# Ends of the 8-head graph-attention layers: free buffers and late denominators; the last projection's rows finished in groups of four

## The chip, the cores and the metric

The kernel runs on one core of a Trainium2 chip. A core has five engines with queues of their own: PE multiplies matrices into PSUM, DVE and ACT do elementwise work, POOL and SP here mainly issue DMA transfers (POOL also clears buffers). The metric is the device time of one launch in microseconds; lower is better. The median of three runs of the kernel before is 3410.56 us (3410.44 to 3414.77).

## The reference

Four layers follow each other on x (3327 rows, 512 columns) with one 0/1 matrix adj of 3327 x 3327. Each is x = layernorm(x + layer(x)) over the columns.

- Layers 0, 2 and 3 are graph attention with 8, 8 and 4 heads. For every head Wh = x W; the logit of row i against row j is leaky_relu(f1[i] + f2[j]), where f1 and f2 are products of Wh with two vectors; where adj[i, j] is 0 it is masked; softmax over j; the head's result is the softmax times Wh. Layers 2 and 3 end with elu.
- Layer 1 is a mean over neighbours: of each row's neighbours the first 64 in index order are kept, their rows are averaged and projected, passed through leaky_relu, set to 0 where a row has no neighbour, and added to leaky_relu of another projection of x.

```python
e = leaky_relu(f1[:, :, None] + f2[:, None, :], 0.2)
h = softmax(where(adj > 0, e, -9e15), axis=-1) @ Wh            # layers 0, 2, 3
keep = (A > 0) & (cumsum(A > 0, axis=1) <= 64)                 # layer 1
xj = leaky_relu((keep @ X) / max(cnt, 1) @ W_nb.T + b_nb)
x = layernorm(x + layer(x))
```

## The kernel before

The rows are padded to 26 tiles of 128 (NT = 26), in two halves of 13 (HALF). The transposed mask stays in SBUF as fp8 for the whole launch.

**The order of work.** PE's instructions keep the order in which the program writes them. On the other engines a scheduler orders the instructions when the program is built, except where `tc.keep_in_program_order` pins one. An engine runs its queue in order, so an instruction that waits holds everything behind it. Tiles come from pools with a number of buffers (`bufs`): a tile with the same name or tag waits until an older buffer has been read for the last time.

**An attention layer.** It begins with a projection (`project1`: four transposes of a row tile, copy `xT` on ACT; `project2`: 16 matmuls into `pw`, then `vt` on DVE, stored in DRAM as v). `prepare` and `cut` make the columns and rows of logits of one half, `rows` loads rows of logits broadcast over the partitions (`rb`, on POOL's queue). Then `unit` runs 8 times: for each half of the output columns i (1664 of them) and each slot s of 4 (two heads in an 8-head layer, one in layer 3). It walks over 26 tiles j: per head DVE makes the weights `t` (L402), ACT makes the fp8 tile `y` (L405), PE adds `t` times v into four banks `po` (L425), and for pairs of j adds the denominators into two banks `pd` (L377). At its end `po` goes to `ob`; `transposed` turns it by quads of four tiles (QUADS: 4, 4, 4, 1) on PE, copies it to `hb` on ACT (L457; two buffers) and stores it in DRAM as hd through SP (L458). That work is a list of jobs, one of which is taken at each j of the next unit. After the last unit what is left of the list is run at once; these are the ends of the layers.

**The denominators.** Per half, after slot 3 of the 8-head layers, the sums in `pd` lie in rows by piece and head. DVE transposes them in blocks of 32 (L486, L487) and adds pieces (`red`, L491). SP writes `red` to DRAM in four transfers with 32-byte pieces (`dd`, L495) and reads it back by row in one (`pes`, L498). `finish_sums` (L507 to L513, pinned for 8 heads) combines them on DVE into `rec`, the reciprocals. Layer 3 does so too, but after its very last unit it copies `pd` to `db`, and PE multiplies by a matrix of pieces (`sums`, L533) instead.

**Finishing rows.** `finish_steps` loads the row tiles h (from hd) and xr (the layer's input, always on POOL's queue), divides (L180), with elu takes exp on ACT (L185) and adds (L191, L192), otherwise adds (L194); `norm_rows` takes the statistics of all tiles of a group (L152, L153), the square root on ACT (L154), and scales on ACT (L161). Exp and square root use different tables of ACT, and a change of function between them brings a table load. The first two tiles are finished in the hook `ending`, ahead of the last `den` of the last unit.

**Sage (layer 1).** In its first part, for groups of two tiles, `finish` of the next group is issued, then `step1` (transposes L682, `xT` L684) and `step2` (16 matmuls `pz`, `pi`, L690 and L693; three bf16 parts of z, two in SBUF as `zs`, the third in DRAM as zd). In the second part `zl` is read back by 13 loads. For every block of 256 rows and every two tiles j, `pk` receives the carries `cy` (ACT, L762), PE adds the running count (L770), DVE makes the kept mask `kt` (L774), and PE adds three matmuls per tile j into `acc` (L809). `output` makes y (L782 on) with the counts `cnt`, which come from `cb`, a read of the counts in DRAM (L743 to L745), and the next layer's weights `wsb` are loaded on POOL (L730) for its projection, which begins behind tile 0. The counts `ctd` are made during layer 0 by `count_jobs` (`ct` L629, L632; `nb` L635).

**Layer 3's projection** (`third`) finishes rows in groups of two, each group's steps in one go ahead of the projections of the group before.

**Layer 0's projection** loads `xt` in three buffers on POOL's queue, interleaved with the loading of the mask; at t = 14 it runs `prepare`, `rows` and `cut` of half 0.

## Time and profile before

| what | us |
|---|---|
| median of three runs | 3410.56 |
| the profiled execution | 3407.9 |
| its span | 3406.2 |
| PE busy | 3262.8 (96%) |
| DVE busy | 2695.3 (79%) |
| ACT busy | 2351.4 (69%) |
| POOL busy | 214.7 (6%) |
| layer 0: projection, attention, end (from the start of the span) | 0 to 143, to 960.6, to 988.3 |
| sage: projections, turn, main part | to 1172, to 1193, to 1754 |
| layer 2: start, attention, end | to 1793, to 2562.7, to 2583 |
| layer 3: projection, attention, tail | to 2706, to 3380, to 3406.2 |

The profile is of one execution, and all its times are counted from the start of its span. A line such as L402 is a line of the kernel before. A busy PE is no proof of PE at its peak: its matmuls overlap, and their recorded ends are modelled, so the records of a stage are compared with records of the same shape in a stage where PE waits for nobody. PEld is PE's loading of weights, which runs beside the matmuls. A name with q (SPq) is the engine's own queue while it issues a transfer; `dd<-red` behind DMA is the transfer itself, from issue to landing. "A <- B" in a list of waits means that A stood idle until B had ended.

### The profile page before, as it was taken

To read this page: it belongs to the slowest core of one execution; us is meant where nothing else is said; L and a number is where in the kernel's file an instruction comes from. 1 tells how busy PE (TensorE), PEld (TensorE's weight loads), DVE (VectorE), ACT (ScalarE), POOL (GpSimd) and SP (SyncE) were. 2 spreads that over 40 slices of the span, in tenths; PEclk is the share of its full clock that TensorE was granted. 3 is DMA by queue.
4 is the path that set the end of the run, shared out by engine and by line. 5 is a ranking of instruction groups with operands and counts; after the bars stand their busy time and mean duration, and the time that the engine had idled before them with its cause. 6 is when DMAs were issued, how large, how long until landed. Compare 5 with 4: busy or idle time off the path is not lost.

```text
span 3406.2 us, 47019 instructions
## 1 busy us (share of the span) xinstructions
PE 3262.8 (96%) x18423; PEld 1631.0 (48%) x18423; DVE 2695.3 (79%) x2630; ACT 2351.4 (69%) x2128; POOL 214.7 (6%) x344
## 2 busy tenths in 40 slices
PE   8899999999989899999989999999997999999997
PEld 7544344444434345555544444444445754445453
DVE  5799999999967544444449999999997766668886
ACT  2388999999943233333338999899996755559885
POOL 3100000000010111111110000000001000000000
PEclk9899999999989999999999999999998999999998
DMA  9544111110143443333320111211107411122311
GB/s 372 214 127 123 52 49 53 42 49 28 38 123 128 116 111 87 90 85 85 85 81 26 41 50 48 56 44 47 35 25 225 169 41 42 41 51 79 95 42 48
DMA packets 313365, 284.65 MB, mean 84 GB/s; under 512 B 134253, under 2 KB 248631, under 8 KB 313144
## 3 DMA queue, kind: packets, MB, share of 16 engines
q1 hardware_dynamic: 280584, 170.27, 16.9%
q0 software_dynamic: 27040, 103.70, 9.5%
q10 hardware_dynamic: 5520, 7.69, 0.7%
q8 instruction: 145, 2.38, 0.3%
q14 instruction: 76, 0.62, 0.1%
HBM read 212.22 MB, written 69.35 MB: 83 GB/s over the span
## 4 chain that ended last, share of the span: by engine, by line
PE 79%; issue 7%; DVE 6%; DMA 4%; ACT 2%; POOL 0%; SPq 0%; ACTq 0%; POOLq 0%; DVEq 0%
PE po L425 49%; PE acc L809 9%; PE pd L377 7%; PE pw L268 5%; DVE t L402 4%; PE pz L690 3%; PE pi L693 3%; DMA raw<-in_adjT_dram 2%; ACT y L405 1%; PE pt L453 1%; DMA cy<-ctd 1%; PE pk L770 1%; PE pt L258 0%; PE pa L1022 0%; DVE mask L593 0%
## 5 line engine op out<-in xcount | busy, mean ns | idle before, releaser
L402 DVE SCALAR_TENSOR_TENSOR t<-rb,qc,mask 128x1664 f32<-128x1664 f32 x1040 | 1959.9, 1957 | 167.7 <-PE po L425 150.1
L405 ACT ACTIVATE y<-t,bi,sc 128x1664 fp8e4<-128x1664 f32 x1040 | 1771.1, 1766 | 317.3 <-PE pd L377 304.4
L425 PE MATMUL po<-t,vj 128*64 128x448 f32 (+3 forms) x8320 | 1924.6, 520 | 25.0 <-DVE t L402 22.3
L425 PEld LDWEIGHTS po<-t,vj 128*64 128x64 f32 (+1 forms) x8320 | 848.3, 148 | 978.2 <-issue 689.7
L809 PE MATMUL acc<-zs,kt 128*128 128x512 bf16 x1352 | 405.1, 382 | 0.0
L809 PEld LDWEIGHTS <-kt 128*128 128x128 fp8e4 x2028 | 199.1, 98 | 250.8 <-issue 9.5
L268 PE MATMUL pw<-wsb,xT 128*128 128x264 f32 (+1 forms) x1248 | 299.8, 395 | 9.2 <-DVE vt L274 7.5
L762 ACT CAST pk<-cy 128x512 f32<-128x512 bf16 x169 | 98.9, 587 | 294.5 <-DVE kt L774 251.1
L377 PE MATMUL pd<-y,sden 128*32 128x448 fp8e4 (+1 forms) x4160 | 259.4, 342 | 8.2 <-ACT y L405 8.2
L268 PEld LDWEIGHTS pw<-wsb,xT 128*128 128x128 f32 x1248 | 240.4, 196 | 53.4 <-issue 5.0
L809 PE MATMUL acc<-zl,kt 128*128 128x512 bf16 x676 | 257.8, 381 | 4.0 <-DMA zl<-zd 4.0
L774 DVE SCALAR_TENSOR_TENSOR kt<-pk,mask 128x512 fp8e4<-128x512 f32 x169 | 116.0, 687 | 99.7 <-PE pk L770 99.7
L377 PEld LDWEIGHTS <-sden 128*32 128x32 bf16 x4160 | 117.6, 96 | 160.3 <-issue 137.6
L274 DVE TENSOR_TENSOR vt<-pw,dc 128x256 f32<-128x256 f32 x156 | 59.0, 418 | 141.2 <-ACT dc L269 137.1
L356 POOL DMA_DIRECT2D rb<-r x40 | 21.9, 548 | 1617.0 <-DVE t L402 1604.5
L272 ACT COPY rc<-pw 128x8 f32<-128x8 f32 (+1 forms) x78 | 12.7, 163 | 138.7 <-PE pw L268 136.2
L690 PE MATMUL pz<-wn,xT 128*128 128x512 f32 x208 | 97.4, 613 | 10.1 <-ACT xT L684 10.1
L693 PE MATMUL pi<-wl,xT 128*128 128x512 f32 x208 | 93.5, 592 | 0.0
L659 POOL DMA_DIRECT2D cy<-ctd x91 | 67.9, 746 | 338.4 <-ACT pk L762 310.2
L782 DVE SCALAR_TENSOR_TENSOR y<-acc,cnt,bnb 128x512 f32<-128x512 f32 x26 | 19.5, 751 | 85.9 <-PE acc L809 85.9
L593 DVE TENSOR_SCALAR mask<-raw 128x832 fp8e4<-128x832 int32 (+2 forms) x90 | 53.1, 598 | 40.4 <-DMA raw<-in_adjT_dram 40.1
L154 ACT ACT_TABLE_LOAD x45 | 57.7, 1283 | 37.3 <-DVE mv L153 36.7
(177 smaller groups left out, 1661.6 us busy)
## 6 DMA issues: line engine op xcount, KB each, us to landing
vj<-v SPq DMA_DIRECT2D x312, 128.0 KB
rb<-r POOLq DMA_DIRECT2D x40, 832.0 KB, 4.6
raw<-in_adjT_dram SPq DMA_DIRECT2D x67, 416.0 KB
cy<-ctd POOLq DMA_DIRECT2D x78, 256.0 KB, 3.9
h<-hd SPq DMA_DIRECT2D x61, 256.0 KB
v<-vt SPq DMA_DIRECT2D x50, 256.0 KB
hd<-hb SPq DMA_DIRECT2D x48, 256.0 KB
xr<-x POOLq DMA_DIRECT2D x45, 256.0 KB, 3.2
```

The costliest lines, as they stand in the source:

```text
L268: nc.tensor.matmul(pw[e][:, :FW + H], xT[:, c, :], wsb[:, c, e, :], start=c == 0, stop=c == FC - 1)
L274: nc.vector.tensor_tensor(vt[:, hs, :], pw[e][:, :FW].rearrange("p (h d) -> p h d", d=D), self.dc[:, t, hs].rearrange("p (h e) -> p h e", e=1)
L377: nc.tensor.matmul(pd[c][32 * kk:32 * kk + 32, :w_], lhsT, rhs, start=(kk, c) not in seen, skip_group_check=final is not None, stop=last a ...
L402: nc.vector.scalar_tensor_tensor(t, rb[k], self.qc[:, j, h:h + 1], mask[:, j, i0:i0 + IW], op0=ALU.max, op1=ALU.mult)
L405: nc.scalar.activation(y, t, AF.Sigmoid, bias=self.bi[:, j, h:h + 1], scale=self.sc[:, j, h:h + 1], saturate=False)
L425: nc.tensor.matmul(po[c][k * D:(k + 1) * D, :z - a_], vj[:, j % 2, k * D:(k + 1) * D], ts[k][:, a_:z], start=j == 0, stop=j == NT - 1)
L659: nc.gpsimd.dma_start(out=cy[:, :n, :], in_=ctd[t:t + n, b * GW:(b + 1) * GW] .rearrange("(o t) i -> o t i", o=1).to_broadcast([P, n, GW]))
L690: nc.tensor.matmul(pz, xT[:, c, :], wn[:, c, :], start=c == 0, stop=c == FC - 1)
L693: nc.tensor.matmul(pi, xT[:, c, :], wl[:, c, :], start=c == 0, stop=c == FC - 1)
L762: nc.scalar.copy(pks[k % 2], carry[b, t // 4 * 4][:, t % 4:t % 4 + 2, :])
L774: nc.vector.scalar_tensor_tensor(kt, pk, NEIGHBOURS, mask[:, t:t + 2, i0:i0 + GW], op0=ALU.is_le, op1=ALU.mult, saturate=False)
L809: nc.tensor.matmul(acc, kts[t][:, s * P:(s + 1) * P], zs(t, c) if c < 2 else zl[:, t, :], start=t == 0 and c == 0, stop=t == NT - 1 and c ...
```

## The change

It has eight parts; line numbers with "after" are of the changed kernel.

1. `norm_rows` is split into `norm_steps`: the statistics of a tile follow its own addition, the square root and scaling follow for the group. `ending` receives the attention's pool: the xr tiles of the first two rows take buffers of the tag "hb", and in layer 2 the exp tile has two buffers.
2. In the last unit of an 8-head layer the last `hb` takes a buffer of "vj", and the third quad's takes that of "db".
3. Half 0 of the 8-head layers makes its denominators by PE: ACT copies `pd` to `db` in four copies, 13 matmuls follow as a job (`sums`), and two jobs later DVE's `reciprocals`.
4. Where the way over DRAM remains (half 1 of the 8-head layers; layer 3), `dd` is written in one transfer as it lies, and `place` reads it back with 16 transfers of 32-byte pieces. At the ends these go into `late`: in sage `place` is issued at t0 = 4 on SP's queue and `finish_sums` at t0 = 8, in layer 3's projection at groups k = 2 and 3. Within layer 3 `place` goes on POOL's queue at job 2 and `finish_sums` some jobs later. The columns rc are first copied into rec, and the first transpose is pinned.
5. `ct` is copied by ACT instead of DVE, and `nb` reads `ct` instead of PSUM.
6. In sage, `cy` has three buffers and two carries are loaded ahead; `cb` and `cnt` move into the first part; `finish` of the next group is issued after `step1` of the group's first tile; for tile 0 the third matmuls (`zl`) follow after all others; `wsb` is loaded on SP behind them.
7. Layer 3's projection finishes rows in groups 2, 2, 3, 4, 4, 4, 4, 3 and spreads their steps between the projections; h has 12 buffers for 10, xr 8 for 6.
8. Layer 0's projection has five `xt` buffers; `cut` comes at t = 14 as before without `rows` ahead of it, and `rows` comes at t = 20.

```diff
-    def norm_rows(pool, ys, t0):
-        n = len(ys)
+    def norm_steps(pool, ys, t0, n):
...
-                xr = pool.tile([P, F], F32, name="xr", bufs=xbufs)
+                xr = xpool.tile([P, F], F32, name="xr", tag="hb") if xpool else \
+                    pool.tile([P, F], F32, name="xr", bufs=xbufs)
...
+        def add_up(s):
+            add(s)
+            if not parts:
+                parts.extend(norm_steps(pool, ys, t0, n))
+            parts[0](s)
+
         steps.append(load)
         for s in range(n):
-            steps += [lambda s=s: divide(s), lambda s=s: add(s)]
-        steps.append(lambda: norm_rows(pool, ys, t0))
+            steps += [lambda s=s: divide(s), lambda s=s: add_up(s)]
+        steps.append(lambda: parts[1]())
...
-                ending()
+                ending(sp)
...
-                hb = sp.tile([P, 4, P], F32, name="hb")
+                if HS == 2 and half == 1 and s == NS - 1 and n < 4:
+                    hb = vp.tile([P, n, P], F32, name="hb", tag="vj")
+                elif HS == 2 and half == 1 and s == NS - 1 and s0 >= 8:
+                    hb = sp.tile([P, 4, P], F32, name="hb", tag="db", bufs=1)
+                else:
+                    hb = sp.tile([P, 4, P], F32, name="hb")
...
-            if not (final and s == NS - 1):
+            by_pe = HS == 2 and half == 0 or final and s == NS - 1
+            if not by_pe:
...
-                dd = dram.tile([IW, 2, 2 * NS], F32, name=f"dd{self.li}{half}{s}")
-                for kk in range(4):
-                    i_, w_ = (0, WA) if kk < 2 else (WA, WB)
-                    nc.sync.dma_start(out=dd[i_:i_ + w_, kk % 2, :].rearrange("(b i) x -> i b x", i=32),
-                                      in_=red[32 * kk:32 * kk + 32, :w_ // 32].rearrange("p b o s -> p b (o s)"))
-                pes = sp.tile([P, HALF, 2, 2, NS], F32, name="pes", tag="red", bufs=1)
-                nc.sync.dma_start(out=pes.rearrange("p q k o s -> p q (k o s)"),
-                                  in_=dd.rearrange("(q p) k x -> p q (k x)", p=P))
+                dd = dram.tile([P, WA // 32, 2 * NS], F32, name=f"dd{self.li}{half}{s}")
+                nc.sync.dma_start(out=dd, in_=red.rearrange("p b o s -> p b (o s)"))
+                held = []
+
+                def place(pool=sp, tag="red", eng=nc.gpsimd):
+                    pes = pool.tile([P, HALF, 2, 2, NS], F32, name="pes", tag=tag, bufs=1)
+                    held.append(pes)
+                    for kk in range(4):
+                        q0, nq = (0, NA) if kk < 2 else (NA, HALF - NA)
+                        src = dd[32 * kk:32 * kk + 32, :4 * nq].rearrange("i (q m) x -> m i q x", m=4)
+                        for m in range(4):
+                            eng.dma_start(out=pes[32 * m:32 * m + 32, q0:q0 + nq, kk % 2]
+                                          .rearrange("p q o s -> p q (o s)"), in_=src[m])
+                nc.vector.tensor_copy(rec[:, t0:t0 + HALF, hs], self.rc[:, t0:t0 + HALF, hs])
...
-                at = 6 if half == 0 or s < NS - 1 else len(jobs)
+                if end:
+                    self.late = [lambda pool: place(pool, "pes", nc.sync), lambda pool: finish_sums()]
+                    return jobs
                 if final and s > 1:
-                    return [nothing] * 5 + [finish_sums] + jobs[2:]
-                return jobs[:at] + [finish_sums] + jobs[at:]
+                    return [nothing, nothing, place, nothing, nothing, nothing, finish_sums] + jobs[2:]
+                jobs += [nothing] * max(0, 7 - len(jobs))
+                return jobs[:2] + [place] + jobs[2:7] + [finish_sums] + jobs[7:]
...
-                nc.vector.tensor_copy(db[64:, c * (WB // 2):(c + 1) * (WB // 2)], pd[c][64:, :WB // 2])
+                (nc.scalar.copy if HS == 2 else nc.vector.tensor_copy)(
+                    db[64:, c * (WB // 2):(c + 1) * (WB // 2)], pd[c][64:, :WB // 2])
...
+            if not final:
+                return jobs[:2] + [sums, nothing, reciprocals] + jobs[2:]
...
-                nc.vector.tensor_copy(ct[:, :w_], held["p"][:, :w_])
+                nc.scalar.copy(ct[:, :w_], held["p"][:, :w_])
...
-                nc.vector.tensor_scalar(nb[:, :w_], pn[:, :w_], 0.0, None, op0=ALU.is_equal, saturate=False)
+                nc.vector.tensor_scalar(nb[:, :w_], ct[:, :w_], 0.0, None, op0=ALU.is_equal, saturate=False)
...
-                tc.tile_pool(name="sg_c", bufs=2, reuse_waits="tile") as cyp:
+                tc.tile_pool(name="sg_c", bufs=3, reuse_waits="tile") as cyp:
...
+            load_carry()
             load_carry()
...
+                    if t0 in (4, 8):
+                        prev.late.pop(0)(fp)
+                    if t0 == 8:
+                        tc.keep_in_program_order(
+                            nc.vector.tensor_scalar(cnt[:, 0, :], cb, NEIGHBOURS, 1.0, op0=ALU.min, op1=ALU.max))
...
                         xT = step1(y)
+                        if s == 0 and t0 + 2 < NT:
+                            ahead = finish(fp, xin, prev, t0 + 2, 2, 6, nc.sync if t0 else nc.gpsimd)
...
-                load_wide(wsb, wsrc, nc.gpsimd)
...
-                            for c in range(3):
+                            for c in range(2 if t0 + s == 0 else 3):
...
+                        if t0 + s == 0:
+                            for t in range(NT):
+                                nc.tensor.matmul(acc, kts[t][:, :P], zl[:, t, :], start=False, stop=t == NT - 1)
+                            load_wide(wsb, wsrc, nc.sync)
...
+                cuts = [0, 2, 4] + list(range(7, NT, 4)) + [NT]
+                bounds = list(zip(cuts, cuts[1:]))
...
+                    if k in (2, 3):
+                        L2.late.pop(0)(fp)
+                    load_group()
+                    steps = groups[k + 1][1] if k + 1 < len(groups) else []
+                    each = -(-len(steps) // max(1, t1 - t0 - 1))
+                    for s, y in enumerate(groups[k][0]):
...
                         xT = L3.project1(pp, ps, y, t)
+                        for _ in range(min(each, len(steps))):
+                            steps.pop(0)()
                         if pend:
                             L3.project2(pp, bank, wsb, *pend)
...
-                xt = pp.tile([P, F], F32, name="xt")
+                xt = pp.tile([P, F], F32, name="xt", bufs=5)
...
                     L0.prepare(pp, 0)
+                    L0.cut(pp, 0)
+                if t == NT - 6:
                     L0.first_rows = L0.rows(rp, 0, 0)
-                    L0.cut(pp, 0)
...
-                     ending=lambda: ends.extend(finish(f0, x, L0, 0, 2, 2)))
+                     ending=lambda sp: ends.extend(finish(f0, x, L0, 0, 2, 2, nc.sync, None, sp)))
...
-                             ending=lambda: ends.extend(finish(f2, x2, L2, 0, 2, 2)))
+                             ending=lambda sp: ends.extend(finish(f2, x2, L2, 0, 2, 2, nc.sync, None, sp, 2)))
```

## The prediction

> **What bounds the kernel now.** I read the table of windows first, cut at the stages of the program. Columns: window, length, busy time (and records) of PE, PEld, DVE, ACT and POOL, granted clock, DMA share, GB/s.
>
> ```profile
> core 0: us, PE busy (x) PEld busy (x) DVE busy (x) ACT busy (x) POOL busy (x), PEclk, DMA share, GB/s
> 143.00:560.00 417.00, 401.09 (x2964) 173.65 (x2966) 414.84 (x276) 372.02 (x250) 4.30 (x8) 0.99 0.26 78
> ...
> 960.60:988.30 27.70, 13.02 (x39) 6.21 (x37) 11.92 (x30) 6.45 (x13) 5.54 (x10) 0.75 0.75 226
> ...
> 1172.00:1193.00 21.00, 11.10 (x35) 4.03 (x34) 6.43 (x13) 4.61 (x8) 6.37 (x8) 0.75 0.91 225
> ...
> 2562.70:2583.00 20.30, 8.08 (x39) 6.36 (x37) 10.59 (x21) 10.47 (x16) 7.30 (x13) 0.75 0.92 255
> 2583.00:2654.30 71.30, 58.48 (x274) 48.45 (x275) 64.11 (x162) 53.73 (x115) 8.26 (x16) 0.90 0.74 249
> ```
>
> The first row is half 0 of layer 0's attention: DVE is busy 414.84 of 417 us, with `t` (L402, 1957 ns each, 1040 times) as its work. Time taken from DVE there comes off the span; PE (401 of 417) follows. Layer 2 is alike; layer 3's attention is bound by PE (670.99 of 674). The short rows are the joints: the end of layer 0 (27.7 us, PE working 13.0), the turn inside sage (21.0), the end of layer 2 (20.3) and the slow start of layer 3's projection. The clock of 0.75 says that PE also pays after a pause: 16 `pw` matmuls take 5.73 us instead of 3.67.
>
> Then the chain of waits at layer 0's end (start, us, what):
>
> ```profile
> 964.56 6.68 SPq L495
> ...
> 971.30 3.01 SPq L495
> ...
> 974.35 2.84 DMA dd<-red
> ...
> 977.25 2.52 DMA pes<-dd
> ```
>
> The denominators' way through DRAM, SP stuck behind its four `dd` writes, holds DVE until 979.8. The waits of that stretch, and after them those of the two other joints (longest wait last):
>
> ```profile
> DVE rec L507 <- DMA pes<-dd: 15.6, 1, 15.6
> PE pz L690 <- ACT xT L684: 10.1, 1, 10.1
> ACT hb L457 <- DMA hd<-hb: 9.5, 1, 9.5
> ```
>
> ```profile
> ACT pk L762 <- DVE kt L774: 14.5, 5, 7.1
> DVE cnt L743 <- DMA cb<-ctd: 6.7, 1, 6.7
> PE acc L809 <- DMA zl<-zd: 4.0, 1, 4.0
> ```
>
> ```profile
> PEld pt L258 <- ACT h L161: 22.6, 4, 10.8
> DVE rec L507 <- DMA pes<-dd: 5.9, 1, 5.9
> ```
>
> ACT stands in `hb`, for a buffer whose store sits behind those writes, so `xT` and `pz` are late; in sage a read of counts (`cb`) stops DVE ahead of `kt`; at layer 2's end the first tiles come late from ACT.
>
> **What the Trainium skill says.** "TensorE: Matmul & The Clock Gate", What's actually happening: PE falls to half clock after an idle window of about 3.4 us and needs a busy one to return; the 5.73 us agree, so each joint closed is worth a few us beyond its idle time. "VectorE: DVE Perf Modes", The perf-mode tier table: a tensor_scalar with a PSUM operand goes at 2x at most, from bf16 in SBUF at up to 4x; `nb` from PSUM takes 680 ns here, and my estimate for it from SBUF is 0.4 us. "ScalarE: Activation LUTs", What ACT_TABLE_LOAD costs: about 1283 ns; this trace's mean of 45 loads is 1283. "DMA: Bandwidth & Descriptors", Specifications: under 512 B a transfer is read-modify-write. Here the old `pes` read, 1664 pieces of 64 B, landed in 2.52 us, so small pieces alone don't make it slow.
>
> **The change, part by part** (gain positive).
>
> Layer 0's projection: `xt` gets 5 buffers for 3, `cut` is issued before `rows`, and the four-head loads of `rows` go from step 14 to step 20. Before, PE waited 5.83 us at tile 19 for an `xt` that landed 11.85 us after its issue, then ran 16 `pw` in 5.56 instead of 3.73: 7.7 us in all. DMA is full there (share over 0.9 from 10 to 125), so a part will only move: +4 (0 to 8).
>
> Layer 0's attention, DVE-bound. Half 0's denominators leave DVE: transposes at 0.59 to 0.64 and reduces at 0.5, 3.5 us in sum; the reciprocal part stays. `ct` copies go to ACT: 6 at 0.60 start to start and 2 at 0.28, 4.1 us. `nb` reads SBUF: 6 times some 0.25 and little for the small ones, 1.7 us. Sum 9.3. What is added: ACT gets some 1.9 us of copies and 4.1 us of `ct` (372 busy of 417, so it has the room: four `y` take 7.06 of the 7.45 us that four `t` take), PE 13 matmuls (about 2.8 us: the like at L533 run from 3377.5 to 3380.3). If ACT's lag reaches the six `t` buffers the cover is gone, and the gain falls to 4. I take +8 (4 to 10). Layer 2 has only the 3.5: +3 (1 to 4).
>
> Layer 0's end. The order of the built program shows: one `dd` write for four; no `hb` waits for a store; `xr` loads early; sixteen small `pes` reads only in sage, in two parts of eight around the loads of h for tiles 4 and 5. Yet tiles 0 and 1 already have their sums, and what starts tile 2 is `pt` at 988.31. On DVE, work of tile 4 (L205 on its h) now stands ahead of the statistics of tile 3 and of the rs steps for tiles 2 and 3. h of tile 4 is on SP behind eight `pes` reads: `dd` from 964.5 lands near 968, eight issues at the 0.36 to 0.54 us of SP's rows bring 972, the load lands by 977 to 980, then four row steps of 0.6, the statistics, ACT's sqrt (table loads of 1.28 before it) and `h` at 0.81: 985 to 988. ACT's two table loads also stand before the last `y`, 2 us lost. So +3 (-3 to +9); from the removed waits alone it would be 10.
>
> Inside sage. `cb` and the counts move into the projections, where PE is full and DVE busy 125 of 184; `wsb` moves behind tile 0, where it is wanted 10 us later at the earliest; two carries are preloaded; tile 0's 26 `zl` matmuls go last, so the 4.0 us for `zl` are covered by 52 others. The 21 us hold about 7 of useful PE work, 14 are to be won; what stays is PE's own pitch, 1.51 us per two tiles with `zl` (starts of `kt` at 1199.19, 1200.71, 1202.22: seven matmuls of 0.216) and 1.08 without, if the carries come: a `cy` for four tiles takes 3.9 us at the median, more while the 13 `zl` loads fill DMA (0.91), with three buffers for two. I take 1.5 a pair for that: 13 x 1.5 from 1174.5, then 26 `zl` matmuls, 5.6 us, give 1199.6, against 1207.6 now; at 1.08 it would be 1194, at 2.0 1206. +7 (2 to 12).
>
> Layer 2's end and layer 3's projection. The first tile's sqrt waits no more on two `hb` stores (2.4 each) but on ACT's queue (three `hb` at 0.59, a table load, sqrt, two `h` at 0.81): `pt` at 2568 for 2575.4. Tile 2 needs DVE rows of tile 7, whose h comes on SP behind `dd` and six reads: about 2583 for 2590.5. From there the groups of 2, 2, 3, 4... end the waits and half-clock stretches up to tile 4 (2602.5 before), and at the pitch of 3.95 us the lead stays: tile 4 at 2594, 7 at 2606, 11 at 2625.5 (2634.3 before), 15 at 2646 (2654.3 before); after it PE is full (50.95 of 51.7) in both. Fewer table switches (two a group, 8 groups for 13) take 10 x 1.28 off ACT, hidden behind PE. DVE in that window stays near 64 of 71 us and is next in line. +9 (4 to 16).
>
> Layer 3's attention: three sets of 16 `place` reads on POOL, some 16 x 0.55 = 9 us of issue and the landing, with six slots (about 19 us at 3.2 us a slot) before DVE wants them. PE has three `t` (9 us) in hand. -1 (-4 to +1).
>
> Moved at no cost: rc's copy into rec and the pinned transpose sit where DVE waited 15.6 us; were that cover gone, under 1 us. Sum: 4 + 8 + 3 + 7 + 3 + 9 - 1 = 33. The profiled execution took 3407.9 (span 3406.2) and would take 3375; the median of the runs, 3410.6, stands 2.7 above it: 3377.
>
> **Rivals.**
> 1. The joints close altogether: 10 at the end of layer 0, 11 in sage, 16 in layer 2's end and the projection, 7 from `xt`, with 11 of attention: 55, so 3355. For it: the quoted waits are all taken away. Against: DVE's order puts work of later tiles ahead of nearer ones at both ends.
> 2. Only the DVE work is won. The same waits come back as waits for h behind `pes`, and DMA at a share of 0.9 in the joints hands the lateness on: 11 + 4 + about 4, so 3392. For it: at every joint the queues hold more DMAs than before (32 in the two ends).
> 3. Slower. The places are two ends. Sixteen `pes` reads stand in SP's queue with h of tiles 4 to 7 around and behind them. If each takes 2.67 us, as the four `dd` writes did at the end of layer 0 (10.69), h(4) comes 21 us late and h(6) 43 us; sage's projection uses a tile in 7.1 us, so it stands still about 28 us an end: -56 against the +33, so about 3433. It decides above some 1.9 us a read, where the stalls eat the 33. Against: the same kind of write took 0.52 in mid-attention, and the old read of as many bytes 0.36.
> 4. The changes do next to nothing, the gains of attention going to ACT: 3408.
>
> **Chances and range.** Forecast (3364 to 3388 is its own range) 0.57, rival 1 0.14, rival 2 0.17, rival 3 0.08, rival 4 0.04. The range reaches over rival 1 to rival 2's upper part: 3352 to 3400. About 0.2%, 6.8 us, is what can be told from no change: faster 0.88, same 0.04, slower 0.08.
>
> **What would show it.** DVE's time between the two halves' same points in layer 0 shorter by about 9 us; no wait of `hb` on its store; `rec` without a wait for `pes` of several us; tile 2's `pt` of sage 22 to 28 us after the last `pd`; tile 0's `y` in sage some 28 us after the last `pi`; the first `pt` of layer 3 about 5 us after the last `pd`, tile 11's about 63. Wrong would be: SP in `pes` above 1 us each, DVE waiting for h(4) or h(7) for 10 us, ACT ahead of DVE as what ends PE's waits in attention, or PE below 0.95 in layer 3.

## The result, and the profile after

The changed kernel takes 3404.43 us (median of four runs, 3402.6 to 3404.83) against 3411.16 (3410.44 to 3414.77) for four runs of the kernel before beside it: a ratio of 0.9977 (0.996 to 0.9994). The forecast was 3377, with a range of 3352 to 3400. The sign is right; of 33 us some 3 to 7 came. The profiled execution took 3404.83, with a span of 3403.1 against 3406.2.

First the windows of the kernel after, cut at the joints as those of before (columns: window, length, busy time and records of PE, PEld, DVE, ACT and POOL, granted clock, DMA share, GB/s):

```profile
core 0: us, PE busy (x) PEld busy (x) DVE busy (x) ACT busy (x) POOL busy (x), PEclk, DMA share, GB/s
...
958.20:986.80 28.60, 9.86 (x39) 5.15 (x38) 13.03 (x27) 7.27 (x14) 7.02 (x11) 0.77 0.76 196
1171.10:1192.10 21.00, 15.40 (x56) 6.18 (x56) 10.26 (x16) 7.59 (x13) 6.27 (x9) 0.84 0.87 254
2556.90:2577.20 20.30, 9.25 (x39) 7.08 (x37) 14.04 (x31) 10.84 (x20) 9.94 (x18) 0.77 0.92 318
2577.20:2651.30 74.10, 57.78 (x273) 48.34 (x274) 65.47 (x158) 47.20 (x105) 7.55 (x14) 0.90 0.69 224
```

Only the turn inside sage looks different: PE works 15.40 of 21 us there, 11.10 before. The end of layer 0 is 28.6 us long (27.7 before) with PE at work for 9.86 of them, and layer 3's projection up to tile 15 takes 74.1 for 71.3, at the same clock of 0.90.

The whole span by stage, from both traces (a gain is positive). The last `pd` and the last `pi` are taken by their ends, all other points by their starts; a unit of an 8-head layer has 52 `t`, and the second row ends where half of the last unit is still to come:

| stage | before | after | gain | forecast |
|---|---|---|---|---|
| layer 0: projection, to the first `t` | 143.0 | 144.5 | -1.5 | +4 |
| its attention, to the first of its last 26 `t` | 761.5 | 755.4 | +6.1 | +8 |
| from there to the last `pd`, and on to `pt` of tile 2 | 56.2 + 27.7 | 58.3 + 28.6 | -3.0 | +3 |
| rest of sage's projections | 183.9 | 184.3 | -0.4 | 0 |
| the turn, last `pi` to y of tile 0 | 35.4 | 29.1 | +6.3 | +7 |
| sage, tiles 0 to 12; 12 to 15; 15 to 25 | 260.4; 71.1; 215.2 | 259.1; 74.1; 215.2 | +1.3; -3.0; 0 | 0 |
| layer 2: from y of tile 25 to the first `t` | 18.4 | 21.7 | -3.3 | 0 |
| its attention | 790.0 | 786.6 | +3.4 | +3 |
| its end and layer 3's projection | 132.8 | 135.0 | -2.2 | +9 |
| layer 3: attention; tail | 680.9; 29.8 | 681.0; 30.2 | -0.1; -0.4 | -1; 0 |

The gains sum to 3.2 where the spans differ by 3.1; the rest is rounding. Three stages did as forecast; the two ends, the projections and an untouched stage did not.

**The end of layer 0.** The waits between 955 and 990 (us in total, times, longest):

```profile
PE pt L732 <- ACT h L163: 16.7, 1, 16.7
...
POOL xr L126 <- issue: 10.4, 1, 10.4
...
DVE cnt L771 <- DMA cb<-ctd: 7.8, 1, 7.8
```

The waits of before (`rec` for `pes` 15.6, `hb` for its store 9.5) are gone, as the change means them to be. In their place PE waits 16.7 us for the `h` of tile 2. The chain of waits shows what that `h` waits for:

```profile
961.24 9.84 issue
971.08 0.04 POOLq L126
...
971.64 3.23 DMA xr<-in_x_dram
...
974.96 0.70 DVE h L205
```

The chain runs over POOL, which issues the xr of tile 2 only at 971.64. Its timeline shows it standing between two issues (start, duration, line, tile, and in brackets the idle time before):

```profile
960.67 0.56 POOL L126 DMA_DIRECT2D h<-hd  x1
971.64 0.55 POOL L126 DMA_DIRECT2D xr<-in_x_dram  x1 [10.40 <-issue]
```

The timeline of SP, first at layer 0's end and then at layer 2's, shows the other queue:

```profile
961.74 0.33 SPq L523 DMA_DIRECT2D dd<-red  x1
...
970.81 5.15 SPq L533 DMA_DIRECT2D pes<-dd  x8
976.06 1.01 SPq L126 DMA_DIRECT2D h<-hd  x2
...
2563.69 0.32 SPq L523 DMA_DIRECT2D dd<-red  x1
...
2574.79 3.81 SPq L533 DMA_DIRECT2D pes<-dd  x6
```

At both ends the `pes` reads stand at the head of SP's queue until `dd` has landed, 9.1 and 11.1 us after its issue, and the loads of h stand behind them. A read itself costs 0.64 us (5.15 for eight, 3.81 for six). In layer 3's attention, where the write of `dd` is the same and its reads stand on POOL's queue, the first read could go 2.3 to 3.4 us after the issue of the write (2.31, 2.42 and 3.35 in this trace).

ACT's timeline before the last `pd` shows the two table loads around the square root of tiles 0 and 1, ahead of the last `y`:

```profile
952.94 1.28 ACT L156 ACT_TABLE_LOAD   x1
...
954.54 1.28 ACT L424 ACT_TABLE_LOAD   x1
955.84 1.77 ACT L424 ACTIVATE y<-t,bi,sc 128x1664 fp8e4<-128x1664 f32 x1
```

**The turn.** Its waits in the 21 us from the last `pi`:

```profile
ACT pk L815 <- DVE kt L827: 7.7, 8, 1.5
...
ACT pk L815 <- DMA cy<-ctd: 4.1, 1, 4.1
```

`cnt` for `cb` (6.7) and `acc` for `zl` (4.0) are no more in the list. y of tile 0 comes 29.1 us after the last `pi`.

**The end of layer 2.** The waits from 2556 to 2656:

```profile
PE pt L277 <- ACT h L163: 23.6, 4, 13.6
```

Before, PE's weight loads waited 22.6 us for the same `h`, in four pieces too. By PE's timeline the first `pt` now comes 5.3 us after the last `pd` (12.7 before) and tile 2 26.3 after it (27.7 before); but tile 4 is late again, after another 4.78 us for `h`: 41.6 us after the last `pd` for 39.7. Tile 15 comes 94.4 after it for 91.5.

The forecast gave these points as times of the clock, counted from the last `pd` of the kernel before, at 2562.7. In the changed kernel the last `pd` comes at 2556.9, 5.8 us earlier, so the forecast has to be read by distances from it: 20.3 us for tile 2, 31.3 for tile 4, 83.3 for tile 15. Of the 11.1 us by which tile 15 misses it, 6.0 are there at tile 2 and 10.3 at tile 4. DVE's timeline shows what tile 2 waits for:

```profile
2581.53 0.69 DVE L191 TENSOR_TENSOR h<-h,rec 128x512 f32<-128x512 f32 x1 [2.99 <-DMA h<-hd]
2582.14 0.15 DVE L160 SCALAR_TENSOR_TENSOR rs<-mv,rs 128x2 f32<-128x2 f32 x1
```

The first line is the h of tile 7, which SP issued at 2578.63, behind `dd` and the six reads; the `rs` that tiles 2 and 3 need stands behind it in DVE's order.

### The profile page after: what moved, and what is told of

The parts are those of the page before. It is cut to its first block, busy times and chain, and to the rows that moved or that the text cites. A ratio compares the mean times of both kernels' runs of the same rounds, so it can differ in the third digit from the quotient of the medians.

```text
span 3403.1 us, 47106 instructions
## 1 busy us (share of the span) xinstructions
PE 3252.5 (96%) x18423; PEld 1628.2 (48%) x18475; DVE 2686.8 (79%) x2605; ACT 2343.8 (69%) x2127; POOL 243.6 (7%) x393
## 4 chain that ended last, share of the span: by engine, by line
PE 84%; DVE 5%; issue 4%; DMA 4%; ACT 3%; POOL 0%; SPq 0%; ACTq 0%; DVEq 0%; POOLq 0%
PE po L444 50%; PE acc L863 12%; PE pd L396 7%; PE pw L287 5%; DVE t L421 3%; PE pz L740 3%; PE pi L743 3%; DMA raw<-in_adjT_dram 2%; ACT y L424 1%; PE pk L823 1%; PE pt L472 1%; PE pa L1086 0%; DMA dd<-red 0%; PE pt L277 0%; PE pt L732 0%
## 5 line engine op out<-in xcount | busy, mean ns | idle before, releaser
L444 PEld LDWEIGHTS po<-t,vj 128*64 128x64 f32 (+1 forms) x8320 | 837.8, 148 | 975.4 <-issue 699.1
L863 PE MATMUL acc<-zs,kt 128*128 128x512 bf16 x1312 | 394.8, 382 | 2.4 <-issue 0.4
L863 PE MATMUL acc<-zl,kt 128*128 128x512 bf16 x638 | 242.1, 379 | 0.6
L291 ACT COPY rc<-pw 128x8 f32<-128x8 f32 (+1 forms) x78 | 12.7, 163 | 168.2 <-PE pw L287 168.0
```

The source lines that it names most:

```text
L444: nc.tensor.matmul(po[c][k * D:(k + 1) * D, :z - a_], vj[:, j % 2, k * D:(k + 1) * D], ts[k][:, a_:z], start=j == 0, stop=j == NT - 1)
L863: nc.tensor.matmul(acc, kts[t][:, s * P:(s + 1) * P], zs(t, c) if c < 2 else zl[:, t, :], start=t == 0 and c == 0, stop=t == NT - 1 and c ...
```

## Experiments

The first theory was that holds in queues at the ends eat the gain: the wait for `cb` that the scheduler put on DVE, the `pes` reads ahead of h on SP, and whatever holds POOL. The rival said that one of them does it all, or that DVE's order alone does. Times are medians; n is given where an interval follows, and runs without one are single runs, read by stages. "before" is the kernel before on the same chip.

**One wait on DVE (e1).** Only the third instruction of the counts is pinned to its place.

```diff
-                        nc.vector.tensor_scalar(cnt[:, 2, :], cb, 0.0, None, op0=ALU.is_gt)
+                        tc.keep_in_program_order(
+                            nc.vector.tensor_scalar(cnt[:, 2, :], cb, 0.0, None, op0=ALU.is_gt))
```

> The changed kernel with its third count instruction (cnt, is_gt) pinned in program order like the first, so that it no longer stands on DVE at layer 0's end. It waited 7.76 us for cb there. Theory A (POOL and SP decide): hardly anything moves, because cb still holds POOL for 10.4 us and xr of tile 2 lands at 974.9 as before, with h of tile 4 behind the pes reads; pt of tile 2 at 986.8 moves by less than 1.5 us. Rival (the wait of cnt on DVE is the cause): pt of tile 2 comes 6 to 8 us earlier, near 980.

3403.6 against 3410.41 before; the end of layer 0 takes 28.6 us from the last `pd` to tile 2, as without the edit. The 7.8 us of DVE were not what tile 2 waited for, or not alone.

**The places of `pes` (e2).** The reads are pinned, and `late` comes later: t0 = 8 and 10 in sage, within the projections of tiles 6 and 8 in layer 3.

```diff
-                            eng.dma_start(out=pes[32 * m:32 * m + 32, q0:q0 + nq, kk % 2]
+                            ins = eng.dma_start(out=pes[32 * m:32 * m + 32, q0:q0 + nq, kk % 2]
...
+                            if HS == 2:
+                                tc.keep_in_program_order(ins)
...
-                    if t0 in (4, 8):
+                    if t0 in (8, 10):
...
-                    if k in (2, 3):
-                        L2.late.pop(0)(fp)
...
+                        if t in (6, 8):
+                            L2.late.pop(0)(fp)
```

> The changed kernel with the 16 pes reads of both ends pinned on SP behind the loads of h (sage: issued at t0 = 8, sums at t0 = 10; layer 3: at tiles 6 and 8). Theory A (h of later tiles waits on SP behind pes, which waits for dd to land, 9 to 11 us): at layer 0's end pt of tile 2 comes 2 to 4 us earlier than 986.8 (xr of tile 2 still late through cb); at layer 2's end pt of tile 2 comes near 2579.5 for 2583.2 and the end of the projection 3 to 5 us earlier; in all 5 to 8 us off 3404.4. Rival (DMA is full there at a share of 0.9, so that a load issued earlier lands no earlier): within 1.5 us of the changed kernel at both ends and in all.

3398.38 (n 5), ratio 0.9966 (0.9952 to 0.998). Layer 0's end is 27.1 for 28.6. At layer 2's end tile 2 comes 23.8 us after the last `pd` for 26.3, tile 4 36.7 for 41.6, tile 15 90.9 for 94.4. So the `pes` reads do delay h at layer 2's end, by 2.5 to 5 us at tiles 2 and 4. At tile 15 the 3.5 us are less sure, since profiles with the same code there lie between 92.6 and 94.4 (changed kernel, e1, e9, e11). At layer 0's end the reads hide behind something else. DVE takes the h of tile 7 22.1 us after the last `pd` in e2, where no read stands ahead of it, and 24.6 in the changed kernel; why that load is slow even so was not tried.

**With `cb` moved too (e3).** As e2, and `cb` is read on SP in the group t0 = 8, with the counts at 14; all of it is pinned but the reciprocal of the counts.

```diff
-                nc.gpsimd.dma_start(out=cb, in_=ctd[NT:NT + 1, :].rearrange("o (t p) -> p (o t)", p=P))
...
+                    if t0 == 8:
+                        tc.keep_in_program_order(
+                            nc.sync.dma_start(out=cb, in_=ctd[NT:NT + 1, :].rearrange("o (t p) -> p (o t)", p=P)))
+                    if t0 == 14:
```

> As the run before, and cb is loaded on SP at t0 = 8, pinned, with all uses at t0 = 14, so that POOL has no cb at layer 0's end and DVE no cnt. Theory A: xr of tile 2 lands before 968, pt of tile 2 near 975 to 978 for 986.8, so 9 to 12 us off layer 0's end and 13 to 18 us in all off 3404.4 (about 3388). Rival of full DMA: pt of tile 2 not before 984, in all within 4 us of the run before.

3400.83 (n 8), ratio 0.9973 (0.9962 to 0.9983). Layer 0's end is 24.3, 4.3 us off, far less than expected, and 1.7 are lost again up to tile 12, which e2, the same without the move of `cb`, does not lose. POOL's timeline in e3 says why the gain is small; the issue before this one was at 961.13:

```profile
971.56 0.54 POOL L126 DMA_DIRECT2D xr<-in_x_dram  x1 [9.88 <-issue]
```

POOL stands as long as before, with no `cb` in its queue. That `cb` holds it, which I had taken for granted, is refuted.

**The DVE relief alone (e4).** The kernel before with parts 3 and 5 only: half 0's denominators by PE, `ct` by ACT, `nb` from `ct`.

```diff
+            by_pe = HS == 2 and half == 0 or final and s == NS - 1
+            if not by_pe:
...
-                nc.vector.tensor_copy(ct[:, :w_], held["p"][:, :w_])
+                nc.scalar.copy(ct[:, :w_], held["p"][:, :w_])
...
-                nc.vector.tensor_scalar(nb[:, :w_], pn[:, :w_], 0.0, None, op0=ALU.is_equal, saturate=False)
+                nc.vector.tensor_scalar(nb[:, :w_], ct[:, :w_], 0.0, None, op0=ALU.is_equal, saturate=False)
```

> The kernel before with parts 3 and 5 of the change alone: half 0's denominators of the 8-head layers by PE, ct copied by ACT, nb from SBUF. Theory: in the changed kernel layer 0's attention is 6.0 us shorter up to its last units and layer 2's 3.4, so alone they give 8 to 10 us (0.25 to 0.3%) off 3410.6, about 3401.5, since nothing behind them moves. As the prediction had it: 11. Rival: the gain is given back behind them by the scheduler's order at the joints (as the changed kernel lost 3.3 us at the start of layer 2), so 3 to 6 us.

3398.36 (n 5) against 3410.41 (n 13), ratio 0.9966 (0.9953 to 0.9979). Layer 0's attention gains 6.4 us and layer 2's 3.3, as in the changed kernel, so these parts carry the whole of it. The median gains 12 where the full change gains 6.7; the intervals overlap, and the profiled execution was the slowest of the five (3403.4), with 134.5 us of PE at half clock for 116.4 in the profile of before. What can be said is that the other six parts together bring nothing that can be measured.

**What holds POOL (e5).** In the built program the load of xr for tile 2 waits for SP's store of the last, small `hb`: part 2 put that `hb` into a "vj" buffer, and sage's xr lies over the same memory. Here it takes a "y" buffer instead, at both ends.

```diff
-                    hb = vp.tile([P, n, P], F32, name="hb", tag="vj")
+                    hb = yp.tile([P, n, P], F32, name="hb", tag="y")
```

> The changed kernel, with one line undone in its sense: the small last hb takes a buffer of y instead of vj. In the built program xr of sage's tile 2 lies where vj lay, and waits for the store of that hb; POOL stands 10.4 us there, and so it did without cb (9.9 us). New theory: that memory is what holds POOL, so xr of tile 2 is issued near 962 for 971.6. Taken alone the start of tile 2 gains little, since cnt on DVE still waits for cb until 969.5 and h of tile 4 comes behind pes: pt of tile 2 0 to 3 us earlier after the last pd (28.6 us in the changed kernel). Rival (POOL waits for its own transfers, DMA being full): xr is issued as late as before, within 1 us.

3399.64 against 3409.97 before. POOL's timeline in e5:

```profile
958.35 0.56 POOL L126 DMA_DIRECT2D h<-hd  x1
958.90 0.55 POOL L126 DMA_DIRECT2D xr<-in_x_dram  x1
```

The 10.40 us are gone. The end is still 28.0, 0.6 better: the next holds in the row, DVE at `cb` and h behind `pes`, are left.

**All three holds (e6).** The edits of e1, e2 and e5 together.

```diff
-                    hb = vp.tile([P, n, P], F32, name="hb", tag="vj")
+                    hb = yp.tile([P, n, P], F32, name="hb", tag="y")
...
+                            if HS == 2:
+                                tc.keep_in_program_order(ins)
...
+                        tc.keep_in_program_order(
+                            nc.vector.tensor_scalar(cnt[:, 2, :], cb, 0.0, None, op0=ALU.is_gt))
```

> As the run before, with pes pinned behind the loads of h (both ends) and cnt pinned in its place. Theory of three holds in a row (hb's memory, cnt, pes): all three gone, pt of tile 2 comes 17 to 21 us after the last pd for 28.6. If only the memory mattered it would be as in the run before; if DMA sets the pace, 24 to 28 as with the pins alone (24.3 to 27.1).

3401.6 against 3409.97. The end is 24.9, better by 3.7 but short of what was expected. Now DVE waits 11.2 us in two pieces for the h of the next tiles, and SP spends long on issuing four of them (its timeline in e6):

```profile
964.34 10.98 SPq L126 DMA_DIRECT2D h<-hd  x4
```

The transfer of `cb` is still there: 3328 pieces of two bytes, which landed 9.6 us after its issue.

**And `cb` off that place, and the early square root late (e7).** As e6, with `cb` on POOL's queue in the group t0 = 8, the counts at 14, and the square root of tiles 0 and 1 pinned where the program has it, behind the last `y`.

```diff
+            ins = nc.scalar.activation(rs[:, :n, 0], mv[:, :n, 1], AF.Sqrt, bias=eps)
+            if pinned:
+                tc.keep_in_program_order(ins)
...
+                    if t0 == 8:
+                        tc.keep_in_program_order(
+                            nc.gpsimd.dma_start(out=cb, in_=ctd[NT:NT + 1, :].rearrange("o (t p) -> p (o t)", p=P)))
```

> As the run before, with cb loaded on POOL behind the xr loads of sage, and the first square root of layer 0's end pinned behind the last y, so that ACT loads no tables between two y. Theory: the last pd comes 2.2 us earlier after the last t (56.1 for 58.3 us), tile 2's pt 17 to 21 us after it, layer 3's projection as in the run with pes pinned (3.5 us less than the changed kernel): 10 + 2 + 3.5 off the changed kernel's median of 3404.4, so 3387 to 3391. Rival: the start of sage is won but given back in its first tiles, where DVE catches up: 3395 to 3399, as the pins alone.

3391.14 (n 5) against 3409.97 (n 9), ratio 0.9945 (0.9931 to 0.9958). From the first of layer 0's last 26 `t` to the last `pd` it takes 56.2 us again, for 58.3: the two table loads were these 2.1. The end takes 18.4 us, 10.2 less than after. DVE waits 3.9 us for h where it waited 11.2 in e6, and in SP's timeline of e7 the line of e6 has become

```profile
964.13 6.31 SPq L126 DMA_DIRECT2D h<-hd  x4
```

`cb` moved without the "y" buffer gave 24.3 (e3), the "y" buffer without `cb` moved 24.9 (e6), both 18.4: holds in parallel, of which each one alone hides what the others would give. e7 moved the square root together with `cb`, so their shares of the last 6.5 us are not separated.

**Groups of two (e8).** Layer 3's projection keeps the stepwise finishing but in groups of two.

```diff
-                cuts = [0, 2, 4] + list(range(7, NT, 4)) + [NT]
+                cuts = list(range(0, NT + 1, 2))
```

> The changed kernel with layer 3's rows finished in groups of two throughout (13 groups for 8, so 10 more table loads on ACT), steps spread as in the change. Theory A: the delay of tile 4 (41.6 us after the last pd for 39.7 before, though tile 2 was 1.4 us earlier) comes from the group of three, whose statistics DVE must all have: tile 4's pt 37 to 39.5 us after the last pd, and the rest of the projection as in the changed kernel or up to 3 us shorter. Rival: the delay is that of h behind pes on SP, whatever the groups: tile 4 at 41 to 43, and the end later for the table loads.

3395.92 (single run). Tile 4 comes 36.3 us after the last `pd` (41.6 after, 39.7 before) and tile 15 86.5 (94.4, 91.5). In the window from 2576.0 to 2642.2, which ends with tile 15 as the last row of windows at the top does, ACT is busier (54.52 us in 66.20, for 47.20 in 74.10), since table loads are back, and the stage is shorter all the same. Profiles with the changed kernel's groups and places of `pes` put tile 15 between 91.1 (e5) and 94.4, so its grouping cost 5 to 8 us. That is the grouping as a whole: the edit also changes how far ahead h is loaded, which queue the first of them take and where `pes` stands. Whether working row by row between the projections was good is not shown, since no run undid it alone.

**An untouched stage (e9).** Between sage's last y and layer 2's first `t` no line of the program differs, but the DVE order does. Before, eight steps of `cut` stood in the gap ahead of the last `vt` (DVE timelines, before and then after):

```profile
1763.94 0.39 DVE L332 CAST pc<-dc 128x104 bf16<-128x104 f32 x1
...
1768.62 0.76 DVE L274 TENSOR_TENSOR vt<-pw,dc 128x256 f32<-128x256 f32 x2 [2.56 <-ACT dc L269]
```

```profile
1763.86 0.76 DVE L293 TENSOR_TENSOR vt<-pw,dc 128x256 f32<-128x256 f32 x2 [5.35 <-ACT dc L288]
...
1765.49 0.34 DVE L351 CAST pc<-dc 128x104 bf16<-128x104 f32 x1
```

After, DVE idles 5.35 us and does all of `cut` behind the `vt`, up to the first `t` at 1770.37. e9 writes `rows` behind `cut`:

```diff
-                L2.first_rows = L2.rows(rp, 0, 0)
...
+                L2.first_rows = L2.rows(rp, 0, 0)
```

> The changed kernel with layer 2's piece columns and cut of half 0 written ahead of the load of its first rows, nothing else. In the built program the cut's first copy then stands ahead of the last two vt on DVE, as it did in the kernel before; in the changed kernel it stands behind them. Theory (the scheduler's order of unchanged code cost the 3.3 us at layer 2's start): from sage's last y to layer 2's first t 18 to 19.5 us for 21.7, other stages as in the changed kernel. Rival (the stage is longer for a slower clock or late transfers): 21 to 22.

3400.34 against 3408.51. The stage takes 17.5 us (21.7 after, 18.4 before), so the reordering was the cause; but layer 2's attention gives 2.7 back (789.2 for 786.6), so the net is 1.5. In e9 DVE waits 2.3 us of that attention for PE's `po` ahead of a `t`, which it did not do in the changed kernel: an earlier first `t` is only in part a gain.

**The best of these together (e10).** e7, e8 and e9.

```diff
-                cuts = [0, 2, 4] + list(range(7, NT, 4)) + [NT]
+                cuts = list(range(0, NT + 1, 2))
...
-                L2.first_rows = L2.rows(rp, 0, 0)
...
+                L2.first_rows = L2.rows(rp, 0, 0)
```

> All holds away as before, with groups of two in layer 3's projection and the cut ahead of the rows. Sum over that run (3391.1): 5 to 7 us in the projection (pt of tile 15 85 to 87 us after the last pd for 92.5), 2.5 to 3 at layer 2's start: 3381 to 3384. If the two ends share one limit (DVE in layer 3's projection), so that pinned pes and groups of two do not add: 3386 to 3388.

3379.71 (n 5) against 3408.51 (n 9), ratio 0.9915 (0.9901 to 0.9928): better than both kernels, and near the 3377 that the forecast saw in the change itself. Its windows at the end of layer 0 and in layer 3's projection (columns as at the top):

```profile
955.00:975.40 20.40, 11.37 (x60) 5.57 (x48) 12.53 (x26) 9.83 (x16) 5.30 (x10) 0.97 0.91 301
...
2565.00:2628.30 63.30, 55.38 (x274) 46.56 (x274) 59.18 (x147) 49.23 (x106) 7.52 (x14) 0.95 0.75 250
```

The first of them begins 2.3 us ahead of the last `pd`; the end itself takes 18.1. The last window holds 274 matmul records, as that of before (273 after), in 63.3 us, for 71.3 and 74.1. Against the changed kernel it has won 12.6 us from the first of layer 0's last 26 `t` to tile 2 of sage, 10.7 from the last `pd` of layer 2 to layer 3's first `t`, and 1.6 between sage and layer 2's end. Counted from layer 2's last `pd`, tile 2 comes at 23.7, tile 4 at 33.6, tile 11 at 62.2 and tile 15 at 83.6: from tile 11 on the forecast (63 and 83.3) is met, by a kernel that finishes its rows in twos.

**Layer 0's projection as it was (e11).** The changed kernel with part 8 undone.

```diff
-                xt = pp.tile([P, F], F32, name="xt", bufs=5)
+                xt = pp.tile([P, F], F32, name="xt")
...
-                    L0.cut(pp, 0)
-                if t == NT - 6:
                     L0.first_rows = L0.rows(rp, 0, 0)
+                    L0.cut(pp, 0)
```

> The changed kernel with part 8 undone: three xt buffers, rows loaded at t = 14 ahead of cut. The start of the first t was 142.4 to 145.5 in nine profiles with part 8 (143.9 in the mean, run by run) and 143.0 in the kernel before, 143.6 with only DVE's relief. Theory (DMA is full there and the part moves no bytes away, so nothing is won): 142 to 145. As the prediction had it: part 8 wins 4, so 146.5 to 149 here.

3401.22 against 3408.51. The first `t` is at 143.6; in the changed kernel and its nine variants that keep part 8 it lies between 142.4 and 145.5. Part 8 brings nothing that shows. PE's waits for `xt` in the later half of the stage go from 6.5 us (this run) to 2.7 (changed kernel); in the latter it waits 9.5 for `vt` instead (5.3 before).

## Why the prediction was wrong

**Right.** The turn: +7 forecast, 6.3 measured, y of tile 0 29.1 us after the last `pi` where "some 28" was named, with the two waits gone that were to go (how the 6.3 divide between them and the other moves of part 6 was not tried). Layer 2's attention: +3 and 3.4. The first `pt` of layer 3 5.3 us after the last `pd`, where 5 was named. Layer 3's attention: -1 and -0.1. The sixteen small reads: 0.30 to 0.77 us each on SP, well below the 1.9 from which the slower rival would have decided; what they cost is mostly the wait for `dd` at the head of the queue. Luck: tile 2 of layer 3 came at 2583.2 of the span where 2583 was forecast, but only since all of it had moved 5.8 us forward; by its distance from the last `pd` it was 6.0 us late.

**"From there the groups of 2, 2, 3, 4... end the waits ... the lead stays" (+9, measured -2.2).** This is the largest miss, 11 us, and two steps of the prediction failed in it. The first comes before the groups: "whose h comes on SP behind `dd` and six reads: about 2583". The order was right; the landing of `dd` and of h behind it was priced too low. At layer 0's end `dd` was to land some 3.5 us after its issue ("from 964.5 lands near 968"). It took 9.1 us there and 11.1 at layer 2's end, while 2.3 to 3.4 in layer 3's attention shows that the forecast price is met elsewhere. e2, with no read ahead of h, wins 2.5 of the 6.0 us at tile 2; the other 3.5 stay with h itself, for which DVE waits there too (2.0 us ahead of tile 7's). Why `dd` and h land so late at the ends was not tried; DMA's share is 0.76 and 0.92 in the two windows.

The second step is the groups. From tile 2 to tile 4 the forecast has 11.0 us, and 15.3 were measured. In a group no row is scaled until the last has its statistics. The DVE timeline of the kernel after shows those of tiles 4 and 6, and the reciprocal of their three square roots:

```profile
2589.41 0.17 DVE L153 BATCH_NORM_AGGREGATE mv<-st 128x2 f32<-128x6 f32 x1
...
2593.47 0.17 DVE L153 BATCH_NORM_AGGREGATE mv<-st 128x2 f32<-128x6 f32 x1
...
2595.66 0.17 DVE L157 RECIPROCAL rs<-rs 128x3 f32<-128x3 f32 x1
```

Tile 4 was ready at 2589.4 and waited 4.1 us for tile 6 (two table loads of ACT, at 2593.8 and 2595.8, follow before it is scaled). Against the kernel before, both counted from the last `pd`, there is a lead of 1.4 us at tile 2 where 7.4 was forecast, and at tile 4 a lag of 1.9. The forecast counted the table loads saved, which lie beside other work, and not the longer way of the first row of a group. e8 has the term: in groups of two tile 2 to tile 4 takes 10.8 us, and 5 to 8 us are won up to tile 15. The delay by the `pes` reads, which the forecast had up to tile 2, reaches the tiles behind it as well (e2: 5 us at tile 4).

**"`xr` loads early" and what starts tile 2 (+3, measured -3.0, the edge of its range).** The two table loads before the last `y` were forecast as 2 us and measured 2.1. The rest missed two holds: `xr` was read as early from its place in the order, while its memory made it wait 10.4 us for a store; and `cnt`, whose third instruction is not pinned, was counted under the projections "where PE is full" while the scheduler put it at the very start of them, 7.8 us of DVE. h of tile 4 "by 977 to 980", 16 to 19 us after the last `pd` of before, came to DVE 23.1 us after the last `pd`, since SP stood for `dd` until 12.6 us after it, where the forecast had 7.3: the same step as at layer 2's end. The naive 10 us were there to be had: e7 gives 9.3 of them against the 27.7 before.

**Layer 0's projection (+4, measured -1.5).** The wait for `xt` was lessened and moved to `vt`, in a stage whose DMA is full (share over 0.9). The prediction said that such a part "will only move" and still gave half; e11 says none.

**Layer 0's attention (+8, measured 6.1).** The term was too large, not wrong. The mechanism is shown by e4. Of the 9.3 us counted off DVE the trace shows 8.5 (759.3 us busy before between the two points, 750.8 after), while DVE's idle time there rose from 2.3 to 4.7 us, waits for PE's `po` and ACT's `y` among it: as DVE gets shorter, others begin to hold it.

**What wasn't in the sum.** Layer 2's start lost 3.3 by a new order of untouched instructions, which the order of the built program would have shown, had it been read at that place; e9 settles the cause. Sage's tiles 12 to 15 lost 3.0; e4, which has the old code there, takes 73.9 us for them as well, so this isn't the change. In seven of the thirteen profiles, that of the changed kernel among them, PE has a stretch of half clock of 3.4 us there, near 1485 to 1505, and the stage takes 73.5 to 74.5; in the six without, that of the kernel before among them, it takes 71.1 to 72.8. Half of such a stretch is 1.7 us; the rest is the spread between profiles.

Together: 11.2 at layer 2's end and projection, 6.0 at layer 0's end, 5.5 in its projection, 3.3 and 3.0 in the two stages without a forecast and 1.9 in attention are 30.9; the other stages did 1.1 better than forecast, and that makes the 29.8 us between 33 and the 3.2 of the table. Of the rivals the fourth (3408) lies nearest by its number but not by its reason: the gains of attention did not go to ACT. The second was right in its reason, that "the same waits come back as waits for h behind `pes`"; it still counted the new grouping as no loss. Both were given too little.

## What to carry to other kernels

When a change takes waits away by giving tiles other buffers, ask for every new buffer who uses that memory next and on which queue that user stands: here a small store's buffer stopped a load of the next stage for 10 us, and the profile names it only as "issue". Where several queues feed the same next tile, their holds lie side by side, so one repair shows nothing (e1, e5) and the last one shows them all (e7); judge such a repair by its own wait, not by the time. Rows that the next stage awaits one at a time were better finished in twos than in threes and fours here, though that brought more table loads, which lay beside other work. And a forecast of where a tile will be is best written as a distance from an event of its own stage: as a time of the clock it can come true because the stages ahead got shorter.

## What the runs showed of the hardware

- PE's half-clock stretches come in multiples of 3.4 us (6.8, 10.2, 13.7 and 17.1 in these traces), which agrees with the Trainium skill, "TensorE: Matmul & The Clock Gate", What's actually happening, where the window is 3413 ns and runs freely. They fall at other places from profile to profile, and their sum goes from 100 to 135 us over the thirteen profiles (116 before, 117 after), so a stage of unchanged code differs between single profiles, in part by them: tiles 12 to 15 of sage by up to 3.4 us (71.1 to 74.5). A stage's difference below that says little.
- A read of 6.5 KB in 3328 pieces of two bytes (`cb`) lands 10.3 us after its issue at the end of layer 0, where DMA's share is 0.96 while it runs, and 6.9 us at a quieter place (e7, share 0.44); 256 KB of xr take 3.2. With it beside them, four loads of h took 10.98 us of SP's queue in e6 and 6.75 in e2, without it 6.31 in e7 and 4.78 in e3. The pairs e6 and e7, and e2 and e3, differ in more than `cb`, so this points to it and does not prove it.
- In the changed kernel's profile a write of 128 rows (`dd`) lands 2.3 to 3.4 us after its issue in layer 3's attention and 9.1 and 11.1 us after it at the ends of layers 0 and 2; what waits for it at the head of a queue holds all behind it as long.
